# A two-layer graph kernel: layer 1's buffers laid over early-ending ones, off-diagonal sources first, denominators in pairs, P three deep

## The chip, the core and the metric

The kernel runs on one core of a Trainium2 chip. The time is that of the device for one launch, in microseconds (us); a kernel is timed in several runs and the median is given. A profile of one run shows what each engine did: PE (TensorE; PEld is its weight loads), DVE (VectorE), ACT (ScalarE), POOL (GpSimd) and SP (SyncE, which here only issues transfers).

## What is computed

There are N = 2708 nodes with D = 256 features. Layer 0 is two steps of a top-p attention and of a random walk, with residuals and two layer norms. It stands ahead of the change and is not given here. Layer 1 is a graph attention with H = 4 heads of FO = 64 features:

```python
Wh = jnp.einsum('nd,hdo->nho', x, W)
s_i = jnp.einsum('nho,ho->nh', Wh, a_src)
s_j = jnp.einsum('nho,ho->nh', Wh, a_dst)
e = leaky_relu(s_i[:, None, :] + s_j[None, :, :], 0.2)
mask = (adj_with_unit_diagonal != 0)[:, :, None]
attention = softmax(where(mask, e, -inf), axis=1)
h_prime = jnp.einsum('ijh,jho->iho', attention, Wh)
x = layernorm(x + h_prime.reshape(n, h * fo))
```

For each target node i, every source node j is weighted by exp(leaky_relu(s_i + s_j)) where the adjacency isn't zero. The diagonal always counts.

## The kernel before, in words

The 2708 nodes are 22 tiles: 16 of 128 rows and 6 of 110. `fast_layer0` computes layer 0 with an order of instructions written out by hand. As each tile t of layer 0's result is ready, `sources(t)` multiplies it with the weights and leaves the scaled values of that tile as a DRAM tensor `vd[t]` (line 160), and in SBUF `sb` = exp(s_j), `tj` = exp(-0.8 s_j) and `s_src` = s_i. Each pool of layer 0 is opened where it is first used, and all are closed before layer 1. (A slower general path for layer 0 follows under a condition that isn't met with these inputs.)

`layer1` uses that exp(leaky_relu(s_i + s_j)) divided by exp(0.2 s_i) is exp(s_j) · max(exp(0.8 s_i), exp(-0.8 s_j)), and that the divisor cancels in the softmax. So for a source tile j and head h

P_h = max(r_h, tj_h) · mask,

with r = exp(0.8 s_i) spread over all partitions, one column for each target. Values are v(j) transposed times P, denominators `bj(j)` transposed times P, with `bj` = sb repeated 32 times.

Targets come in three spans of 8, 8 and 6 tiles (1024, 1024 and 660 columns). In each span a loop goes over all 22 source tiles:

- `neighbours` (lines 1131 to 1143): the `bar` transfer (L1136) brings the 128 rows of the transposed adjacency, issued on SP; ACT takes the Sign (L1137); if tile j is itself in the span, POOL sets the diagonal to one (L1140, L1141); ACT takes the Square (L1142). Four `bar` buffers.
- Four DVE operations make P for the four heads (L1189), in the pool `pj` with two buffers for each head.
- PE adds the values to `acc[0]` and `acc[1]` (L1197), two heads at a time side by side in column tiles 64 wide. It then adds the denominators to `acc[2]` (L1204), four heads side by side in column tiles 32 wide. In the profile each of these matmuls leaves two records.

At the span's end, ACT and DVE copy the sums to SBUF (L1212 to L1214). `settle` then finishes the span's tiles one by one: three PE transposes (L1152, L1153), the reciprocal and the product on DVE (L1155, L1159), the residual on POOL (L1164), the layer norm on DVE and POOL (L125 to L132), and the transfer to the output. It stands in the program at the third source (j == 2) of the next span; the last span's comes at the end. `targets(g + 1)` (PE transposes L1122, ACT exponentials L1126) makes the next span's r at j == 11.

The values of all 22 sources are loaded from `vd` at the head of `layer1`, issued on ACT (L1103); POOL makes the 22 `bj` (L1104).

Two things set the order around the change. A scheduler puts each engine's instructions in order from the program's order and from its dependences. And the pools set addresses: a buffer of layer 1 lies over some buffer of layer 0, and what writes it first waits for that one's last reader. Before the change, `bar` lies over the buffers `xa1` and `hh` of layer 0's last sums and norms, r over `yw` and `ba`, v and bj over weights and row buffers, and the transposes' `aux` banks over those of `att` and `walk`.

Of the kernel before, what the change touches and what calls it, by code (L numbers as in the profile page):

```python
# [8 lines left out]
F32 = mybir.dt.float32  # L9
# [5 lines left out]
PSUM = bass.MemoryType.PSUM  # L15
# [30 lines left out]
def kernel(  # L46
# [407 lines left out]
    def fast_layer0():  # L454

        l0 = ExitStack()
        w0 = l0.enter_context(tc.tile_pool(name="w0", bufs=1))
        rowp = l0.enter_context(tc.tile_pool(name="rowp", bufs=2))
        keep = l0.enter_context(tc.tile_pool(name="keep", bufs=1))
        HN = N // 2  # L460
# [11 lines left out]
        b_sb = w0.tile([P, D], F32, name="b_sb")  # L472
        heldp = l0.enter_context(tc.tile_pool(name="heldp", bufs=HELD))
        tmp = heldp.tile([P, D], F32, name="xa1")
# [41 lines left out]

        qT = keep.tile([P, N], F32, name="qT")
        yw = keep.tile([P, NT, D], F32, name="yw")
        ba = keep.tile([P, NT, D], F32, name="ba")
        rinv = keep.tile([P, NT], F32, name="rinv")  # L520

        dram = l0.enter_context(tc.tile_pool(name="dram", bufs=1, space=bass.MemoryType.DRAM))
        c1 = [dram.tile([P, D], F32, name=f"c1_{t}") for t in range(NT)]
        c2 = [dram.tile([P, D], F32, name=f"c2_{t}") for t in range(NT)]

        sortp = l0.enter_context(tc.tile_pool(name="sortp", bufs=1))
        finp = l0.enter_context(tc.tile_pool(name="finp", bufs=2))
        ep = l0.enter_context(tc.tile_pool(name="ep", bufs=3))
        wk = l0.enter_context(tc.tile_pool(name="wk", bufs=1))

        kT = [wk.tile([P, HN], F32, name="junk"), keep.tile([P, HN], F32, name="kT1")]
        tpp = l0.enter_context(tc.tile_pool(name="tpp", bufs=3))
        adjp = l0.enter_context(tc.tile_pool(name="adjp", bufs=3))
        ps_lg = l0.enter_context(tc.tile_pool(name="ps_lg", bufs=2, space=PSUM))
        ps_tr = l0.enter_context(tc.tile_pool(name="ps_tr", bufs=2, space=PSUM))
        ps_at = l0.enter_context(tc.tile_pool(name="ps_at", bufs=1, space=PSUM))
        ps_wk = l0.enter_context(tc.tile_pool(name="ps_wk", bufs=1, space=PSUM))

# [551 lines left out]
    def layer1():  # L1090
        l1 = ExitStack()
        keep = l1.enter_context(tc.tile_pool(name="keep1", bufs=1))
        pp = l1.enter_context(tc.tile_pool(name="pp", bufs=2))
        GT = 8
# [3 lines left out]

        v = [keep.tile([P, H, FO], F32, name=f"v{t}") for t in range(NT)]
        bj = [keep.tile([P, H, 32], F32, name=f"bj{t}") for t in range(NT)]  # L1100
        for t in range(NT):
            m = rows[t]
            nc.scalar.dma_start(v[t][:m].rearrange("p h o -> p (h o)"), vd[t][:m])  # L1103
            nc.gpsimd.tensor_copy(  # L1104
                bj[t][:m], sb[:m, t, :].unsqueeze(2).to_broadcast([m, H, 32])
            )

        rp = l1.enter_context(tc.tile_pool(name="rp", bufs=2))
        adjp = l1.enter_context(tc.tile_pool(name="adjp1", bufs=4))
        pj = l1.enter_context(tc.tile_pool(name="pj", bufs=2))  # L1110
        ps_v = l1.enter_context(tc.tile_pool(name="ps_v", bufs=1, space=PSUM))
        ps_u = l1.enter_context(tc.tile_pool(name="ps_u", bufs=2, space=PSUM))

# [57 lines left out]
        for g, span in enumerate(spans):  # L1171
# [5 lines left out]
            ]  # L1177
            for j in range(NT):
                k = rows[j]
                if j == 2 and due:  # L1180
                    settle(*due)
                if j == NT // 2 and g + 1 < len(spans):
                    r_next = targets(g + 1)
                mask = neighbours(g, j)
                at = dict(start=(j == 0), stop=(j == NT - 1), skip_group_check=True)
                pts = []
                for h in range(H):
                    pt = pj.tile([P, GW], F32, name=f"pt{h}")
                    nc.vector.scalar_tensor_tensor(  # L1189
                        pt[:k, :gw], r[:k, h, :gw], tj[:k, j, h : h + 1], mask,  # L1190
                        op0=ALU.max, op1=ALU.mult,
                    )
                    pts.append(pt)
                    if h % 2 == 1:
                        for c, (c0, w) in enumerate(cuts):
                            for q in range(2):
                                nc.tensor.matmul(  # L1197
                                    acc[h // 2][c][q * FO : (q + 1) * FO, :w],
                                    v[j][:k, h - 1 + q, :],
                                    pts[h - 1 + q][:k, c0 : c0 + w], **at,  # L1200
                                )
                for c, (c0, w) in enumerate(cuts):
                    for h in range(H):
                        nc.tensor.matmul(  # L1204
                            acc[2][c][h * 32 : (h + 1) * 32, :w],
                            bj[j][:k, h, :], pts[h][:k, c0 : c0 + w], **at,
                        )
            r = r_next
# [61 lines left out]
```

The softmax here doesn't subtract the row's maximum and nothing guards it: scores larger than these inputs give would overflow.

## Time and profile before

| | |
|---|---|
| time, median of 3 runs | 1698.4 us (1698.17 to 1698.85) |
| span of the profiled run | 1697.3 us |
| PE busy | 1620.3 us (95%) |
| DVE busy | 1219.5 us (72%) |
| ACT busy | 767.9 us (45%) |
| POOL busy | 433.6 us (26%) |
| last attention matmul of layer 0 (L187) | starts at 1277.08, 2.75 us |
| last layer norm of layer 0 (L909) | 1289.91, 0.41 us |
| first value product of span 1, 2, 3 | 1312.03, 1439.06, 1576.65 us |
| values of the last source of span 3 | 1671.46 us |

The page gives busy time in 40 slices of the span (tenths), then groups of instructions: line, engine, operation, output and inputs by name, and how many; then busy time and mean ns of one; then the idle time of the engine just ahead of them and what ended most of it. A row of the timeline has start, duration, engine, line, operation, output and inputs, count, and in brackets the idle time before it with its releaser. "SPq" and "ACTq" rows are issues of transfers. In a table by windows each engine's busy time stands with its count, followed by the clock granted to PE, the busy share of the DMA engines and GB/s.

### The profile page before, as it was taken

Reading aid. Unit: us, or ns where it says so; the run is one execution under the profiler, and the core shown is the slowest. Engines: PE = TensorE matmul, PEld = TensorE weight load, DVE = VectorE, ACT = ScalarE, POOL = GpSimd, SP = SyncE. Lnnn points to the kernel's source line nnn. Section 1 sums busy time; section 2 is a strip of 40 time slices with the busy share of each in tenths; the row PEclk is TensorE's granted clock in tenths of the full one; section 3 lists DMA queues with packets and bytes.
Section 4 is the critical chain, followed back from the end, with each engine's and each line's share of the span. In section 5 each row is a group of like instructions: output and inputs, shape, how many; then the busy total and the mean of one; then the engine's idle time right before and its main releaser. Section 6 shows DMA issues by size and latency. Waiting matters only on the chain. (4 is left out here: it accounts for less than half of the span.)

```text
span 1697.3 us, 24178 instructions
## 1 busy us (share of the span) xinstructions
PE 1620.3 (95%) x8306; PEld 1064.8 (63%) x8306; DVE 1219.5 (72%) x3660; ACT 767.9 (45%) x1324; POOL 433.6 (26%) x915
## 2 busy tenths in 40 slices
PE   7999999999999999999999999999985999999895
PEld 4677777777767766777878788777773232322332
DVE  2954554556445029888899999998981989889886
ACT  1333333333333256566666767676723444243231
POOL 0310111111101033223344444453434200430312
PEclk9999999999999999999999999999996999999997
DMA  6211011101111133122223323322204323232231
GB/s 164 72 46 46 27 41 39 43 27 39 40 42 40 44 89 77 48 67 75 71 74 82 85 65 87 80 71 66 68 22 126 100 82 94 87 86 78 73 85 31
DMA packets 153873, 113.89 MB, mean 67 GB/s; under 512 B 39898, under 2 KB 144094, under 8 KB 153742
## 3 DMA queue, kind: packets, MB, share of 16 engines
q1 hardware_dynamic: 146248, 102.41, 22.7%
q0 software_dynamic: 2112, 5.55, 1.0%
q10 hardware_dynamic: 5382, 4.32, 0.9%
q8 instruction: 67, 1.10, 0.3%
q14 instruction: 64, 0.52, 0.1%
HBM read 101.16 MB, written 11.09 MB: 66 GB/s over the span
## 5 line engine op out<-in xcount | busy, mean ns | idle before, releaser
L1189 DVE SCALAR_TENSOR_TENSOR pt<-r,tj,bar 128x1024 f32<-128x1024 f32 (+3 forms) x264 | 297.0, 1187 | 49.8 <-ACT bar L1142 25.5
L619 ACT ACTIVATE junk<-e,minus,rth 128x2708 bf16<-128x2708 f32 (+1 forms) x88 | 233.0, 2648 | 36.1 <-POOL rth L651 35.3
L819 PE MATMUL walk<-xe,blk 128*128 128x257 f32 (+3 forms) x968 | 240.6, 382 | 0.0
L187 PE MATMUL att<-ba,eT 128*128 128x256 f32 (+3 forms) x968 | 234.4, 383 | 5.0 <-ACT eT L178 5.0
L187 PE MATMUL att<-xe,eT 128*128 128x256 f32 (+3 forms) x968 | 233.3, 381 | 4.3 <-ACT eT L178 4.3
L1197 PE MATMUL acc<-pt,v 128*64 128x512 f32 (+3 forms) x1056 | 230.5, 554 | 4.6 <-DVE pt L1189 4.6
L178 ACT COPY eT<-tr 128x512 f32<-128x512 f32 (+5 forms) x264 | 138.2, 538 | 203.3 <-PE tr L172 203.0
L819 PE MATMUL walk<-yw,blk 128*128 128x256 f32 (+3 forms) x968 | 228.0, 381 | 1.8 <-ACT xw L889 1.8
L699 DVE MAX8 cand<-e 128x8 f32<-128x170 f32 (+1 forms) x352 | 89.3, 324 | 171.5 <-ACT e L598 171.5
L819 PEld LDWEIGHTS walk<-xe,blk 128*128 128x128 f32 (+3 forms) x968 | 173.0, 186 | 53.1 <-issue 29.3
L819 PEld LDWEIGHTS walk<-yw,blk 128*128 128x128 f32 (+3 forms) x968 | 176.7, 186 | 41.6 <-issue 11.5
L187 PEld LDWEIGHTS att<-ba,eT 128*128 128x128 f32 (+3 forms) x968 | 171.9, 187 | 33.0 <-ACT eT L178 10.0
L187 PEld LDWEIGHTS att<-xe,eT 128*128 128x128 f32 (+3 forms) x968 | 170.8, 186 | 30.9 <-ACT eT L178 7.2
L598 ACT ACTIVATE e<-lg 128x1024 f32<-128x1024 f32 (+1 forms) x132 | 121.1, 922 | 132.3 <-PE lg L594 132.3
L1197 PEld LDWEIGHTS acc<-pt,v 128*64 128x64 f32 (+1 forms) x1056 | 73.7, 137 | 154.8 <-issue 111.9
L172 PE MATMUL tr<-ident,e 128*128 128x128 f32 (+3 forms) x968 | 140.5, 269 | 4.6 <-ACT xT L580 3.8
L172 PEld LDWEIGHTS tr<-ident,e 128*128 128x128 f32 (+3 forms) x968 | 115.0, 138 | 32.7 <-ACT xT L580 6.1
L1137 ACT ACTIVATE bar<-bar 128x1024 f32<-128x1024 f32 (+3 forms) x66 | 63.0, 956 | 146.0 <-DMA bar<-in_adjT_dram 110.1
L1204 PE MATMUL acc<-pt,bj 128*32 128x512 f32 (+3 forms) x1056 | 124.5, 549 | 0.0
L605 POOL TENSOR_TENSOR fact<-zp 128x1 f32<-128x1 f32 (+1 forms) x44 | 24.9, 566 | 329.2 <-ACT e L598 319.4
L699 DVE MAX8 cand<-scr 128x8 f32<-128x97 f32 (+1 forms) x616 | 101.9, 247 | 0.0
L832 DVE TENSOR_TENSOR xf<-walk,xe 128x257 f32<-128x257 f32 (+1 forms) x22 | 9.4, 427 | 117.4 <-PE walk L819 117.3
(199 smaller groups left out, 2022.1 us busy)
## 6 DMA issues: line engine op xcount, KB each, us to landing
blk<-in_adjT_dram SPq DMA_DIRECT2D x32, 704.0 KB
bar<-in_adjT_dram SPq DMA_DIRECT2D x32, 512.0 KB
blk<-in_adjT_dram SPq DMA_DIRECT2D x32, 330.0 KB
blk<-in_adjT_dram SPq DMA_DIRECT2D x32, 320.0 KB
blk<-in_adjT_dram SPq DMA_DIRECT2D x12, 605.0 KB
bar<-in_adjT_dram SPq DMA_DIRECT2D x12, 440.0 KB
bar<-in_adjT_dram SPq DMA_DIRECT2D x16, 330.0 KB
c<-cs POOLq DMA_DIRECT2D x32, 128.0 KB, 2.1
```

What stands on the lines that cost most here:

```text
L172: nc.tensor.transpose(tr[: rows[t], q, :m], e[:m, off[t] : off[t + 1]], ident[:m, :m])
L178: copy(eT[:k, : len(grp), :m], tr[:k, : len(grp), :m])
L187: nc.tensor.matmul(acc, eT[: rows[t], q, :m], value(t), start=(t == 0), stop=(t == NT - 1),)
L598: nc.scalar.activation(halves[:m, :, c0 : c0 + w], lg[:m, :, :w], AF.Exp, accum_out=zp[:m, n : n + 1],)
L605: nc.gpsimd.tensor_add(z, zp[:m, 0:1], zp[:m, 1:2])
L619: nc.scalar.activation(junk[:m], e[:m], func, scale=rth, bias=minus1[:m], accum_out=acc)
L699: nc.vector.max(cand[:, n, :], src[:m, n * size : min(N, (n + 1) * size)])
L819: nc.tensor.matmul(ac[:m, :w], blk[: rows[j], j - j0, :m], cur[: rows[j], j, 0:w], start=(j == 0), stop=(j == NT - 1),)
L1137: nc.scalar.activation(bar, bar, AF.Sign)
L1189: nc.vector.scalar_tensor_tensor(pt[:k, :gw], r[:k, h, :gw], tj[:k, j, h : h + 1], mask, op0=ALU.max, op1=ALU.mult,)
L1197: nc.tensor.matmul(acc[h // 2][c][q * FO : (q + 1) * FO, :w], v[j][:k, h - 1 + q, :], pts[h - 1 + q][:k, c0 : c0 + w], **at,)
L1204: nc.tensor.matmul(acc[2][c][h * 32 : (h + 1) * 32, :w], bj[j][:k, h, :], pts[h][:k, c0 : c0 + w], **at,)
```

## The change

It has four parts.

1. **Pools laid over each other.** Layer 0 opens its pools in one list, layer 1 in another, in an order that lays layer 1's first buffers over those of layer 0 that end early. After it `bar` lies over `blk` and `e`, r over `e`, P over `ba`, `kT1`, `qT` and `cand`, the v of the first sources over `yw`, and `acc` and `aux` over PSUM banks of `lg`, `walk`, `att` and `tr`. This is to let layer 1 begin while layer 0's last tiles go through their norms.
2. **Off-diagonal sources first.** The first span takes sources 8 to 19, then 0 to 7, then 20 and 21. Those of its own tiles, which need POOL for the diagonal, come later. Each source's v is loaded and its bj copied in the loop, just ahead of its mask, and the load is issued on SP instead of ACT. In the other spans the order stays.
3. **Denominators of two sources in a row.** The values of j and of j + 1 come first, then the denominators of both. PE changes between the two tile widths half as often.
4. **P three deep.** Each head's P has three buffers; with pairs, one source's P is held while the next one's values are computed.

The core of the diff:

```diff
-        w0 = l0.enter_context(tc.tile_pool(name="w0", bufs=1))
-        rowp = l0.enter_context(tc.tile_pool(name="rowp", bufs=2))
-        keep = l0.enter_context(tc.tile_pool(name="keep", bufs=1))
+        heldp, finp, rowp, w0, keep, sortp, adjp, ep, tpp, wk = (
+            l0.enter_context(tc.tile_pool(name=name, bufs=bufs))
+            for name, bufs in (
+                ("heldp", HELD), ("finp", 2), ("rowp", 2), ("w0", 1), ("keep", 1),
+                ("sortp", 1), ("adjp", 3), ("ep", 3), ("tpp", 3), ("wk", 1),
+            )
+        )
+        ps_lg, ps_wk, ps_at, ps_tr = (
+            l0.enter_context(tc.tile_pool(name=name, bufs=bufs, space=PSUM))
+            for name, bufs in (("ps_lg", 2), ("ps_wk", 1), ("ps_at", 1), ("ps_tr", 2))
+        )
...
     def layer1():
         l1 = ExitStack()
-        keep = l1.enter_context(tc.tile_pool(name="keep1", bufs=1))
-        pp = l1.enter_context(tc.tile_pool(name="pp", bufs=2))
+        pp, keep, pj, adjp, rp = (
+            l1.enter_context(tc.tile_pool(name=name, bufs=bufs))
+            for name, bufs in (("pp", 2), ("keep1", 1), ("pj", 3), ("adjp1", 4), ("rp", 2))
+        )
+        ps_u = l1.enter_context(tc.tile_pool(name="ps_u", bufs=2, space=PSUM))
+        ps_v = l1.enter_context(tc.tile_pool(name="ps_v", bufs=1, space=PSUM))
...
-        v = [keep.tile([P, H, FO], F32, name=f"v{t}") for t in range(NT)]
-        bj = [keep.tile([P, H, 32], F32, name=f"bj{t}") for t in range(NT)]
-        for t in range(NT):
+        v, bj = {}, {}
+        for t in reversed(range(NT)):
+            v[t] = keep.tile([P, H, FO], F32, name=f"v{t}")
+            bj[t] = keep.tile([P, H, 32], F32, name=f"bj{t}")
+
+        def stationary(t):
             m = rows[t]
-            nc.scalar.dma_start(v[t][:m].rearrange("p h o -> p (h o)"), vd[t][:m])
+            nc.sync.dma_start(v[t][:m].rearrange("p h o -> p (h o)"), vd[t][:m])
             nc.gpsimd.tensor_copy(
                 bj[t][:m], sb[:m, t, :].unsqueeze(2).to_broadcast([m, H, 32])
             )
-        rp = l1.enter_context(tc.tile_pool(name="rp", bufs=2))
-        adjp = l1.enter_context(tc.tile_pool(name="adjp1", bufs=4))
-        pj = l1.enter_context(tc.tile_pool(name="pj", bufs=2))
...
-            for j in range(NT):
+            order = list(range(NT)) if g else list(range(GT, NT - 2)) + list(range(GT)) + [NT - 2, NT - 1]
+            waiting = []
+            for n, j in enumerate(order):
                 k = rows[j]
-                if j == 2 and due:
+                if n == 2 and due:
                     settle(*due)
-                if j == NT // 2 and g + 1 < len(spans):
+                if n == NT // 2 and g + 1 < len(spans):
                     r_next = targets(g + 1)
+                if g == 0:
+                    stationary(j)
...
-                for c, (c0, w) in enumerate(cuts):
-                    for h in range(H):
-                        nc.tensor.matmul(
-                            acc[2][c][h * 32 : (h + 1) * 32, :w],
-                            bj[j][:k, h, :], pts[h][:k, c0 : c0 + w], **at,
-                        )
+                waiting.append((j, k, pts, at))
+                if n % 2 == 1:
+                    for j, k, pts, at in waiting:
+                        for c, (c0, w) in enumerate(cuts):
+                            for h in range(H):
+                                nc.tensor.matmul(
+                                    acc[2][c][h * 32 : (h + 1) * 32, :w],
+                                    bj[j][:k, h, :], pts[h][:k, c0 : c0 + w], **at,
+                                )
+                    waiting = []
```

The rest of the diff only takes out the lines where the listed pools stood and moves one tensor (`qT`) behind two others.

## The prediction

> **What bounds the kernel now.** I read the page first (shares, then groups), then the busy time by windows, then the timeline of three stretches: the change of layers, the steady loop of layer 1, and the loop while the previous span is settled.
>
> The page, sections 2 and 5 (busy time, mean ns of one, idle time ahead):
>
> ```profile
> PE   7999999999999999999999999999985999999895
> ...
> L1189 DVE SCALAR_TENSOR_TENSOR pt<-r,tj,bar 128x1024 f32<-128x1024 f32 (+3 forms) x264 | 297.0, 1187 | 49.8 <-ACT bar L1142 25.5
> ...
> L1197 PE MATMUL acc<-pt,v 128*64 128x512 f32 (+3 forms) x1056 | 230.5, 554 | 4.6 <-DVE pt L1189 4.6
> ...
> L1204 PE MATMUL acc<-pt,bj 128*32 128x512 f32 (+3 forms) x1056 | 124.5, 549 | 0.0
> ```
>
> TensorE (PE) is full but for the first slice, slices 30 and 31 (42.4 us each: 1231 to 1315, the change from layer 0 to layer 1), 38 (the third span's start) and 40 (the last settle). The 264 P products of VectorE (DVE, L1189) are the second load of layer 1. By windows (us, PE, PEld, DVE, ACT, POOL busy, clock, DMA):
>
> ```profile
> 1280.00:1300.00 20.00, 11.95 (x49) 8.19 (x48) 3.46 (x9) 8.56 (x32) 10.83 (x25) 0.74 0.42 130
> 1300.00:1350.00 50.00, 39.94 (x210) 12.83 (x212) 38.49 (x30) 21.51 (x23) 17.24 (x28) 0.83 0.42 125
> 1350.00:1400.00 50.00, 50.00 (x296) 15.01 (x296) 41.27 (x35) 20.49 (x23) 0.00 (x0) 1.00 0.29 82
> ```
>
> From 1350 PE is the bound; before that it starves. The timeline there shows why:
>
> ```profile
> 1290.40 0.36 SPq L1136 DMA_DIRECT2D bar<-in_adjT_dram  x1
> ...
> 1297.55 11.04 ACTq L1103 DMA_DIRECT2D v<-v  x21
> ...
> 1308.63 1.09 ACT L1126 ACTIVATE r<-aux 128x512 f32<-128x512 f32 x2 [10.67 <-DMA v<-v]
> ...
> 1310.69 2.68 DVE L1189 SCALAR_TENSOR_TENSOR pt<-r,tj,bar 128x1024 f32<-128x1024 f32 x2 [20.37 <-ACT bar L1142]
> ...
> 1312.03 1.97 PE L1197 MATMUL acc<-pt,v 128*64 128x512 f32 x2 [0.78 <-DVE pt L1189]
> ```
>
> The first `bar` transfer leaves at 1290.40, when the last layer norm of layer 0 (DVE L909, 1289.91 + 0.41) has let its buffer go. ACT then issues v loads for 11.04 us, and the last two exponentials `r` (1308.63), the Square of the first mask (1309.60) and the first P (1310.69) queue behind. PE's first value product is at 1312.03; two sources are through at 1326.09.
>
> The steady loop:
>
> ```profile
> 1347.85 3.65 PE L1197 MATMUL acc<-pt,v 128*64 128x512 f32 x16
> 1347.99 4.87 DVE L1189 SCALAR_TENSOR_TENSOR pt<-r,tj,bar 128x1024 f32<-128x1024 f32 x4 [0.56 <-issue]
> 1348.33 0.14 PEld L1197 LDWEIGHTS acc<-pt,v 128*64 128x64 f32 x2 [0.29 <-issue]
> ...
> 1351.43 0.16 PEld L1204 LDWEIGHTS acc<-pt,bj 128*32 128x32 f32 x8 [0.81 <-issue]
> ...
> 1353.28 0.20 PEld L1197 LDWEIGHTS acc<-pt,v 128*64 128x64 f32 x4 [0.84 <-DVE pt L1189]
> ```
>
> A source takes 5.44 us (1347.85 to 1353.28; 5.439 over 1320.65 to 1433.62, after 4.2 for the transposes of `targets`). Weight loads follow each other every 0.4286, twelve steps, 5.143. The other 0.295 lies at the two switches between 64-wide values and 32-wide denominators: there PEld idles 0.81 and 0.84, elsewhere 0.29. DVE needs 4.87, then waits 0.56 for the denominators to free P.
>
> While the previous span is settled (second span, 1450 to 1476):
>
> ```profile
> 1462.27 0.41 DVE L132 TENSOR_SCALAR o<-res,ln_mv,ln_rs 128x256 f32<-128x256 f32 x1 [0.46 <-POOL ln_rs L131]
> 1462.59 0.75 DVE L1159 TENSOR_TENSOR res<-aux,rden 128x256 f32<-128x256 f32 x2
> ...
> 1463.26 1.64 DVE L1189 SCALAR_TENSOR_TENSOR pt<-r,tj,bar 128x1024 f32<-128x1024 f32 x1
> ...
> 1468.80 1.55 DVE L1189 SCALAR_TENSOR_TENSOR pt<-r,tj,bar 128x1024 f32<-128x1024 f32 x1
> ```
>
> One P per 5.5 us, with two tiles settled between: DVE makes 8 P in 26 us, where PE could use 19.
>
> **What the Trainium skill says.**
> - "TensorEngine Tiling (Array Packing)", Key Properties: a change of tiling mode drains TensorE. The trace agrees: 0.147 us per switch.
> - "DMA: Bandwidth & Descriptors", Issuing engines are not separate DMA queues: a different issuing engine saves sequencer time only. The trace shows that time: 11.04 us of ACT for 21 issues, 0.53 each.
> - "TensorE: Matmul & The Clock Gate", What's actually happening: after an idle window TensorE runs at half clock until it has been busy some 3.4 us. It agrees in kind: clock 0.74 and 0.83 in the windows above, and the first source's values take 6.84 against 3.65 (some of this is waiting for P).
> - "SBUF — State Buffer", SBUF: two separate sides: a DVE operation with two SBUF inputs and a GpSimd operation lock each other out. It agrees: a P takes 1.22 alone, 1.317 over the first 24 (POOL masks the diagonal), up to 1.64 at 1463.
>
> **The change, part by part.** Instruction counts are equal but for 22 issues moved from ACT to SP, and the built order is the same up to the last 30 us of layer 0. So layer 0 stays.
>
> *Change of layers.* The masks now lie over buffers (blk, e) whose last readers, transposes of the last e, are through at about 1277, so `bar` leaves some 13 us earlier. In ACT's new order the first Sign and Square stand between r(0) and r(5); what ends last is r(6) and r(7), behind the last cs of layer 0 (ACT, ends 1294.87): two exponentials with their transposes, 1.5 to 2.2, so the first P at about 1296.7, 14 earlier. The first sources are off-diagonal: no POOL work, P at 1.22. The first v lies over yw and also needs the store of v_21 (issued 1294.90; 2.1 to land, as c<-cs): loads start near 1297.5 and land near 1300. PE's first denominators wait for bj, copied by POOL then. Values of source 8 from 1300.3 to 1304.8 (part cold), of 9 to 1308.8, remaining denominators 3 to 3.5: two sources through at 1312.5 against 1326.1. Gain 13.5; 11 if the clock starts cold later, 15 if nothing waits for v.
>
> *Pairs.* v(j) v(j+1) d(j) d(j+1) has 2 switches in 4 segments, where there were 4: 0.147 saved per source. First span: 20 sources, 2.9, less 0.5 while diagonal sources keep DVE at 5.27 against the new period of 5.29: 2.4. Second: 22, 3.2, less 0.7: 2.5. P(j) is now held until d(j), so P(j+3) waits for d(j): in a pair's 10.58 the two denominators end at 9.0 and 10.8, DVE then makes its two sources in 9.74, and values need them at 14.2 and later. I cost this wait at nothing.
>
> *P three deep, settle.* From 1439.06 to 1488.69, six sources took 49.6; six periods (32.6), 5.4 of settle transposes and 1.9 of `targets` make 40: 9.6 lost to DVE. In the new order DVE starts on settle half a source earlier, but spreads it: one tile (1.51) to one P (1.25 to 1.6), ten P over the eight tiles. P runs at 2.8 to 3.2 with one more source in store (5.3 of PE work). Walking it through leaves 2 to 5 lost: gain 4.6 to 7.6, taken 6.1. Third span (660 wide): period 3.618, values 2.37, denominators 1.25, DVE 3.36; seven sources took 44.15 against 30.7. There the order still has two tiles per P but starts two or three P later. Counting the same way eight sources end 42.9 after the start against 47.8: 4.9 with switches; 14 other sources save 0.147 each, 2.1, less 1 on the last six diagonal ones (DVE 3.63 against 3.47): 6.0, from 3 to 8.
>
> *At no cost.* The v issues on SP: it only issues loads, 0.5 each, 22 in 118 us. The bj copies (0.24) lie on POOL behind layer 0's norms and ahead of masks needed a source later. The last settle (about 22 us) is as before: denominators are still last.
>
> Sum: 13.5 + 2.4 + 2.5 + 6.1 + 6.0 = 30.5. 1698.4 − 30.5 = 1667.9, say 1668.
>
> **Rivals.**
> - *DVE becomes the bound* (15%). For it: 5.27 per diagonal source against 5.29, and P up to 1.64 beside POOL. Against: 41.27 of 50 busy off the diagonal. Pairs give nothing, settle its low ends: 13.5 + 4.6 + 3 = 21, 1677.
> - *The start is only half gained* (17%). For it: a source's v comes through a store, SP and a load, one after the other, and PE is cold. Gain 6.5 instead of 13.5: 1675.
> - *Slower* (3%). SP is one queue in order; each v issue stands ahead of its mask, behind a mask load that waits for a buffer. Were every source of the first span to pay one landing (2.1, as c<-cs), 22 × 2.1 = 46 less 30.5: 1714. Against: four masks in flight are 16 us of lead.
>
> **How the numbers follow.** The main case has 65%. Adding low ends (11 + 1 + 1 + 4.6 + 3) gives 20.6, high ends (15 + 2.9 + 3.2 + 7.6 + 8) 36.7: 1662 to 1678. The range reaches from 1660 to 1682, which takes in both milder rivals (1675 and 1677) with some 6 us for a low end more; the slower case and worse mixes are left out. Faster 0.96, within 0.2% 0.01, slower 0.03.
>
> **What would show it.** First `bar` issue near 1277, first P near 1297, first value product near 1300; starts of segments 10.6 apart for two sources with half the 0.8 marks of PEld; six sources at the second span's start in about 43; layer 1's last settle as long as now. Wrong if ACT waits for `bar` or PE for v in the first span, if DVE waits for d at P with POOL beside it, or if layer 0 ends later than 1280.

## The result, and the profile after

The changed kernel takes 1690.3 us (median of 4 runs, 1689.55 to 1690.42), the kernel before 1698.4 in the same session: a ratio of 0.9951, 95% interval 0.9934 to 0.9968. That is 8.1 us faster. 30.5 were forecast, and the time lies outside the range of 1660 to 1682.

The page of the changed kernel, sections 2 and 5. The lines of code have moved by some six: P is L1195, values L1203, denominators L1214.

```profile
PE   7999999999999999999999999999998989899995
...
L1195 DVE SCALAR_TENSOR_TENSOR pt<-r,tj,bar 128x1024 f32<-128x1024 f32 (+3 forms) x264 | 293.0, 1176 | 39.4 <-issue 19.5
...
L1203 PE MATMUL acc<-pt,v 128*64 128x512 f32 (+3 forms) x1056 | 223.1, 549 | 4.0 <-DVE pt L1195 4.0
...
L1214 PE MATMUL acc<-pt,bj 128*32 128x512 f32 (+3 forms) x1056 | 122.5, 545 | 0.9 <-POOL bj L1110 0.9
```

The dip at slices 30 and 31 is nearly gone (it was 8 and 5, it is 9 and 8), but there is a new dip in slice 33, in the middle of the first span, and another in slice 35, where the second span begins; PE was full in both before. By windows:

```profile
1280.00:1300.00 20.00, 13.21 (x62) 9.05 (x61) 6.43 (x12) 14.67 (x40) 9.74 (x17) 0.83 0.37 132
1300.00:1350.00 50.00, 50.00 (x276) 14.71 (x274) 47.37 (x40) 20.67 (x21) 25.72 (x22) 1.00 0.48 142
1350.00:1400.00 50.00, 45.00 (x266) 14.80 (x264) 36.03 (x31) 18.78 (x21) 14.44 (x15) 0.93 0.26 82
```

From 1300 to 1350 PE now works all 50 us instead of 39.9. From 1350 to 1400 it works 45 where it worked 50. The timeline of the change of layers:

```profile
1277.99 0.36 SPq L1136 DMA_DIRECT2D bar<-in_adjT_dram  x1
...
1297.03 33.34 DVE L1195 SCALAR_TENSOR_TENSOR pt<-r,tj,bar 128x1024 f32<-128x1024 f32 x27 [5.97 <-ACT r L1126]
...
1298.59 2.98 PE L1214 MATMUL acc<-pt,bj 128*32 128x512 f32 x8 [0.90 <-POOL bj L1110]
...
1301.50 7.46 PE L1203 MATMUL acc<-pt,v 128*64 128x512 f32 x32
...
1312.45 5.37 PE L1203 MATMUL acc<-pt,v 128*64 128x512 f32 x24
```

The first mask leaves at 1277.99 instead of 1290.40. The first P starts at 1297.03 instead of 1310.69, behind the last r on ACT. Two sources are through at 1312.45 instead of 1326.09. The steady loop of pairs:

```profile
1377.67 0.20 PEld L1203 LDWEIGHTS acc<-pt,v 128*64 128x64 f32 x4 [0.84 <-DVE pt L1195]
1377.67 7.09 PE L1203 MATMUL acc<-pt,v 128*64 128x512 f32 x32
...
1384.69 0.16 PEld L1214 LDWEIGHTS acc<-pt,bj 128*32 128x32 f32 x8 [0.81 <-issue]
1384.69 3.64 PE L1214 MATMUL acc<-pt,bj 128*32 128x512 f32 x32
...
1388.26 0.20 PEld L1203 LDWEIGHTS acc<-pt,v 128*64 128x64 f32 x4 [0.84 <-DVE pt L1195]
```

A pair takes 10.59 us (1377.67 to 1388.26), 5.29 for a source, with two gaps of 0.8 where there were four.

So both the start and the pairs do what they were forecast to do. Where the 22 us went is seen when the timeline is cut into stages. "Two through" is the time at which two sources' values and denominators are done. A span starts with its first value product. The last one ends with its last denominators, less the 0.07 by which neighbouring matmuls overlap in the trace, so that all spans are counted from start to start.

| | two through | rest of span 1 | span 2 | span 3 | last settling to the end |
|---|---|---|---|---|---|
| before | 1326.1 | 113.0 | 137.6 | 98.4 | 22.2 |
| after | 1312.5 | 118.2 | 139.9 | 95.9 | 22.0 |
| difference | −13.6 | +5.2 | +2.3 | −2.5 | −0.2 |

The sum is −8.8, the difference of the profiled spans (1697.3 and 1688.5).

**The first span** loses in one place. One pair, from 1355.92 to 1377.67, takes 21.75 instead of 10.59. It holds the transposes of `targets` (n == 11), which cost 4.2 by themselves; 7.0 are lost. The timeline of that pair:

```profile
1354.35 9.77 DVE L1195 SCALAR_TENSOR_TENSOR pt<-r,tj,bar 110x1024 f32<-110x1024 f32 x8 [0.53 <-issue]
...
1358.78 5.66 POOL L1140 TENSOR_TENSOR bar<-bar,offdiag 128x128 f32<-128x128 f32 x1 [4.10 <-ACT bar L1137]
...
1365.01 1.06 ACT L1142 ACTIVATE bar<-bar 128x1024 f32<-128x1024 f32 x1 [6.31 <-POOL bar L1141]
1365.97 1.07 ACT L1126 ACTIVATE r<-aux 128x512 f32<-128x512 f32 x2
1366.60 1.97 PE L1122 MATMUL aux<-ident,s_src 128*128 128x128 f32 x8 [5.00 <-ACT r L1126]
...
1370.23 0.46 POOL L1140 TENSOR_TENSOR bar<-bar,offdiag 128x128 f32<-128x128 f32 x1 [5.25 <-ACT bar L1137]
1370.37 1.09 PE L1122 MATMUL aux<-ident,s_src 128*128 128x128 f32 x8
...
1376.10 9.65 DVE L1195 SCALAR_TENSOR_TENSOR pt<-r,tj,bar 128x1024 f32<-128x1024 f32 x8 [11.98 <-issue]
```

Read from the bottom of the wait up. PE has two PSUM buffers for the transposes and stands at the third (5.00). ACT hasn't emptied them, since a Square stands ahead of r in its queue, and that Square waits 6.31 for POOL. POOL's small product on the diagonal takes 5.66 instead of 0.46 (1370.23, with no P beside it), and ends as DVE's run of eight P ends (1364.12). In the new order the diagonal sources come at n == 12 and after, just behind `targets`. The wait is 5.00 of the 7.0. The rest comes after it: from 1363.5 to 1370.2 the clock granted to PE was 0.50, where the kernel before has 1.00, and eight transposes take 1.97 at 1366.60 and 1.09 at 1370.37.

**The second and third span** lose while the previous span is settled. The first eight sources of the second span take 59.9 us. Four pairs and 5.4 of transposes make 47.7, so 12.2 are lost, where the kernel before lost about 9.6. In the third span 14.1 are lost (before: 13.4). The timeline of two tiles, second span:

```profile
1457.77 1.26 DVE L1195 SCALAR_TENSOR_TENSOR pt<-r,tj,bar 128x1024 f32<-128x1024 f32 x1
1457.77 1.84 POOL L1164 TENSOR_TENSOR res<-res,xe 128x256 f32<-128x256 f32 x1 [1.19 <-DVE ln_mv L127]
...
1459.88 0.57 POOL L131 TENSOR_TENSOR ln_rs<-ln_ve,minus_half 128x1 f32<-128x1 f32 x1
...
1460.49 0.41 DVE L132 TENSOR_SCALAR o<-res,ln_mv,ln_rs 128x256 f32<-128x256 f32 x1 [1.47 <-POOL ln_rs L131]
...
1461.63 1.25 DVE L1195 SCALAR_TENSOR_TENSOR pt<-r,tj,bar 128x1024 f32<-128x1024 f32 x1
```

One tile and one P take 3.86 us (1457.77 to 1461.63). DVE is idle for 1.47 of them: its `o` waits for POOL's `ln_rs`, which stands behind the next tile's residual, and that takes 1.84 beside a P. Over the eight tiles DVE waits 11.3 us for POOL. In the third span the order is as before, two tiles to one P, and so is the wait, 6.3. In the kernel before it was 6.3 in the second span too. This is the wait of the first of two tiles there:

```profile
1461.39 0.41 DVE L132 TENSOR_SCALAR o<-res,ln_mv,ln_rs 128x256 f32<-128x256 f32 x1 [0.80 <-POOL ln_rs L131]
```

### The profile page after: what moved, and what is told of

Its sections match the earlier page's. It is cut to its first block, busy times and chain, and to the rows that moved or that the text cites. A ratio compares the mean times of both kernels' runs of the same rounds, so it can differ in the third digit from the quotient of the medians.

```text
span 1688.5 us, 24169 instructions
## 1 busy us (share of the span) xinstructions
PE 1614.1 (96%) x8306; PEld 1069.7 (63%) x8306; DVE 1214.4 (72%) x3660; ACT 767.5 (45%) x1324; POOL 455.7 (27%) x915
## 5 line engine op out<-in xcount | busy, mean ns | idle before, releaser
L1195 DVE SCALAR_TENSOR_TENSOR pt<-r,tj,bar 128x1024 f32<-128x1024 f32 (+3 forms) x264 | 293.0, 1176 | 39.4 <-issue 19.5
L1203 PE MATMUL acc<-pt,v 128*64 128x512 f32 (+3 forms) x1056 | 223.1, 549 | 4.0 <-DVE pt L1195 4.0
L1203 PEld LDWEIGHTS acc<-pt,v 128*64 128x64 f32 (+1 forms) x1056 | 73.9, 137 | 145.2 <-issue 110.9
L1214 PE MATMUL acc<-pt,bj 128*32 128x512 f32 (+3 forms) x1056 | 122.5, 545 | 0.9 <-POOL bj L1110 0.9
```

Of the source, the lines that this page charges most:

```text
L1195: nc.vector.scalar_tensor_tensor(pt[:k, :gw], r[:k, h, :gw], tj[:k, j, h : h + 1], mask, op0=ALU.max, op1=ALU.mult,)
L1203: nc.tensor.matmul(acc[h // 2][c][q * FO : (q + 1) * FO, :w], v[j][:k, h - 1 + q, :], pts[h - 1 + q][:k, c0 : c0 + w], **at,)
L1214: nc.tensor.matmul(acc[2][c][h * 32 : (h + 1) * 32, :w], bj[j][:k, h, :], pts[h][:k, c0 : c0 + w], **at,)
```

## The experiments

All kernels here compute what the kernel before does. Each time is a median, with the ratio to the kernel before, timed beside it, and its 95% interval. Stages are as above; the first line repeats the changed kernel. In the names, "np" is without pairs, "away" has the stage with r moved away from n == 11, "deep" has P four deep, "spread" and "light" settle in another way.

| | time, us | ratio (interval) | two through | rest of span 1 | span 2 | span 3 |
|---|---|---|---|---|---|---|
| after | 1690.3 | 0.9951 (0.9934–0.9968) | 1312.5 | 118.2 | 139.9 | 95.9 |
| t_away | 1681.1 | 0.9900 (0.9884–0.9917) | 1311.1 | 111.2 | 138.6 | 95.9 |
| no_pair | 1683.2 | 0.9913 (0.9896–0.9929) | 1310.7 | 113.7 | 139.5 | 94.4 |
| pools_only | 1685.0 | 0.9920 (0.9904–0.9937) | 1312.3 | 113.2 | 137.6 | 98.0 |
| natural | 1688.3 | 0.9940 (0.9924–0.9957) | 1313.1 | 114.7 | 141.5 | 95.9 |
| np_away | 1677.2 | 0.9875 (0.9859–0.9892) | 1312.4 | 113.0 | 133.2 | 94.4 |
| deep4 | 1681.7 | 0.9903 (0.9886–0.9920) | 1311.5 | 117.3 | 139.7 | 89.7 |
| deep4_away | 1676.9 | 0.9874 (0.9857–0.9890) | 1311.7 | 111.2 | 139.9 | 89.7 |
| np_spread | 1676.3 | 0.9873 (0.9857–0.9889) | 1310.3 | 113.0 | 135.3 | 93.1 |
| r_by_tile | 1666.8 | 0.9819 (0.9802–0.9835) | 1310.3 | 109.5 | 132.6 | 89.7 |
| spread | 1674.1 | 0.9858 (0.9842–0.9875) | 1311.5 | 109.5 | 137.0 | 91.5 |
| spread_light | 1656.4 | 0.9756 (0.9739–0.9772) | 1311.0 | 109.5 | 123.7 | 85.8 |
| spread_light_np | 1660.2 | 0.9777 (0.9761–0.9794) | 1312.0 | 111.9 | 126.4 | 83.4 |
| light_only | 1688.1 | 0.9942 (0.9925–0.9958) | 1312.4 | 118.1 | 137.5 | 97.1 |
| deep_light | 1671.9 | 0.9844 (0.9828–0.9861) | 1311.8 | 109.5 | 131.6 | 94.9 |
| hybrid | 1651.9 | 0.9730 (0.9714–0.9747) | 1311.7 | 109.5 | 123.7 | 83.4 |

### Which part of the change did what

**t_away** moves the stage with r to where no diagonal source follows.

```diff
-                if n == NT // 2 and g + 1 < len(spans):
+                if n == (6, 18, 0)[g] and g + 1 < len(spans):
                     r_next = targets(g + 1)
```

> The changed kernel with one edit: the next span's r (the targets stage) is made at n == 6 of the first span and n == 18 of the second, instead of n == 11, so that it stands among off-diagonal sources. Theory A (at n == 11 the transposes stand beside the first diagonal source; POOL's mask waits for DVE's run of P, ACT's Square for POOL, ACT's r for the Square, PE for r): the pair of sources with these transposes takes about 15 us instead of 21.8, the second span starts 7 us earlier, total about 1683. The built order also changes on DVE at the second span's settle: it starts one whole source later and with two tiles to one P; if the settle's loss is set by that order, 3 to 6 more, 1677 to 1680. Rival B (the diagonal sources are simply slow for DVE and POOL): the first span stays as long, total 1690.

The first span became 7.0 us shorter, as theory A had it: the two pairs that share the transposes take 25.4, which is two periods and 4.2. The second span became 1.3 shorter, at its own stage with r, and the third kept its time. The other half of the expectation wasn't put to the test. In the trace DVE settles the second span in the same order as in the changed kernel, one tile to one P from the same source on, and the first eight sources take the same 59.9. So this run says nothing about what that order costs.

**no_pair** takes the pairs back and keeps the three buffers, **pools_only** takes both back.

```diff
-                if n % 2 == 1:
+                if True:
                     for j, k, pts, at in waiting:
```
```diff
-            for name, bufs in (("pp", 2), ("keep1", 1), ("pj", 3), ("adjp1", 4), ("rp", 2))
+            for name, bufs in (("pp", 2), ("keep1", 1), ("pj", 2), ("adjp1", 4), ("rp", 2))
```

> The changed kernel with pairs undone: each source's denominators follow its values at once; P stays three deep. By the cost of a switch, 0.147 us, the period of the first two spans goes back from 5.29 to 5.44 and the third's from 3.47 to 3.62: 9 us dearer in all. Theory A: the stall at n == 11 has nothing to do with pairs and stays, 5 to 7 us. If the settle's loss comes from DVE's order (one tile to one P, which the pairs brought; here it is two tiles to one P, one source later), the second span's first eight sources lose 5 to 7 instead of 12: total about 1692. If the settle's loss doesn't depend on the order: 1699.

> The changed kernel with pairs undone and P two deep again: only the buffers laid over each other, the first span's order and the v loads on SP are left. Two sources should be through near 1312.5 (before: 1326.1), a gain of 13.6. Theory A: at n == 11 the stall costs 5 to 7, total 1690 to 1692. If the stall needs the three deep P or the pairs (a run of eight P on DVE): no stall, total 1685. Settle as in the kernel before (9.6 and 13.4 lost).

Pools, order and v loads alone bring 13.3 of time (1698.3 to 1685.0), more than the whole change. Their spans are those of the kernel before. Three deep P without pairs brings 1.8 more; with pairs on top the kernel is 7 us slower. no_pair shows why it isn't better: its second span loses only 4.3 while settling (ten sources in 64.0 us, against 54.4 + 5.4), where pools_only, with the same order on DVE and one buffer less, loses 9.7. So the third buffer does there what was forecast. In the first span both have hardly a stall, against theory A: the pair with the transposes loses 0.2 in pools_only and 0.8 in no_pair. So the new order alone doesn't make it; it comes with pairs and the longer run of P on DVE. But in its second span no_pair loses 7.0 at n == 11, where that span has its diagonal sources (8 to 15), with PE again 4.86 us behind ACT's r.

**natural** keeps everything but the first span's order.

```diff
-            order = list(range(NT)) if g else list(range(GT, NT - 2)) + list(range(GT)) + [NT - 2, NT - 1]
+            order = list(range(NT))
```

> The changed kernel with the first span's sources in natural order, 0 to 21; all else as changed. Theory A: at n == 11 the sources are off-diagonal, so the stall of 7 us is gone. The start has diagonal sources: P at 1.3 instead of 1.2 and masks through POOL while it makes bj, 1 to 4 us later for the first two sources. Total 1684 to 1688. Rival B (diagonal sources cost the same wherever they stand): 1690 or more.

Two sources are through at 1313.1, only 0.6 later: the start isn't won by the order. Whether by the buffers or by the v loads, which every kernel but the one before issues on SP, no run tells apart. The trace of before gives an estimate. There ACT's last two r and the first Square stand behind 11.04 us of v issues (1297.55 to 1308.59), while the first mask's Sign has ended at 1296.99 and the transposes for those r at 1298.67. Without the issues the first P could have come near 1300.4 instead of 1310.69, which is some 10 of the 13.6; the other 3 would be the earlier masks. The next two pairs take 12.5 and 13.2 instead of 11.7 and 10.6, and the pair with the transposes 14.9. So the order saves 4 us early and, together with pairs, costs 7 at n == 11.

### How much P is in store

**np_away** is no_pair with t_away's edit. **deep4** is the changed kernel with a fourth buffer, **deep4_away** both together.

```diff
-            for name, bufs in (("pp", 2), ("keep1", 1), ("pj", 3), ("adjp1", 4), ("rp", 2))
+            for name, bufs in (("pp", 2), ("keep1", 1), ("pj", 4), ("adjp1", 4), ("rp", 2))
```

> The changed kernel with pairs undone, P three deep, and the next span's r made at n == 6 of the first span and n == 18 of the second. With pairs undone alone, the second span lost 7.0 us at n == 11, where its diagonal sources are (8 to 15), and 4.3 while settling. Theory A (the stage with r must not stand beside diagonal sources): those 7 go, the first span stays, total 1676. Rival B (the 7 us belong to the recovery of DVE after settling, not to the place of r): no gain, 1683.

> The changed kernel with P four deep instead of three, pairs as changed. Theory C (a pair holds one source's P until its late denominators, so that of three buffers no more is in store than of two without pairs): with the fourth the loss while settling falls from 12.2 to about 4 in the second span and from 14 to 9 or 10 in the third, as three deep without pairs has it; total 1690 - 12 = 1678 if the stall at n == 11 stays, 1671 if that goes too. Rival D (the loss while settling is one of DVE's order, or of POOL's locked port): 1688 to 1690.

> Both: P four deep with pairs, r made at n == 6 and n == 18. Theories A and C together: 1681 - 12 = 1669. If depth does nothing: 1681.

np_away came out as theory A had it (1677.2 for 1676): the second span is 6.4 shorter and the third as it was. Under pairs the fourth buffer cuts the loss of settling from 12.2 to 7.1 in the second span and from 14.1 to 7.9 in the third, 11 together, where 12 were expected. So a pair does use up a buffer: three with pairs hold no more in store than two without.

The same numbers give an estimate of what DVE's order costs. In the second span, kernels with two tiles to one P lose 9.7 (pools_only) and 4.3 (no_pair), those with one tile to one P and, so counted, the same store 12.2 (after) and 7.1 (deep4). A buffer is worth 5.1 to 5.4, one source of PE's work, and the order 2.5 to 2.8. No run changes the order alone.

The second span of deep4 took as long as before all the same, 139.7: what settling gave back went at n == 11, where its pair takes 21.3 instead of 16.4. And deep4_away didn't reach 1669. Its second span kept a loss of 7.7, now at n == 18, where no source is diagonal:

```profile
1535.10 0.75 ACT L1137 ACTIVATE bar<-bar 128x660 f32<-128x660 f32 x1 [3.23 <-DMA bar<-in_adjT_dram]
...
1536.54 0.95 ACT L1126 ACTIVATE r<-aux 128x440 f32<-128x440 f32 x2
1537.12 1.73 PE L1122 MATMUL aux<-ident,s_src 110*128 110x110 f32 x8 [4.39 <-ACT r L1126]
...
1550.59 1.72 DVE L1195 SCALAR_TENSOR_TENSOR pt<-r,tj,bar 128x660 f32<-128x660 f32 x2 [8.89 <-issue]
```

PE is at n == 18, ACT already at masks of the next span (660 wide), and r is queued behind one whose transfer hadn't come. POOL plays no part. The stall is one of order on ACT: r stands behind masks that wait for something. On the diagonal that is POOL, here a transfer. That ACT's queue runs further ahead of PE's when more P is in store fits these runs, but was not measured by itself.

**r_by_tile** has four buffers and makes r one tile at a time, so that no third tile's transposes stand right behind those of two others.

```diff
-                if n == NT // 2 and g + 1 < len(spans):
-                    r_next = targets(g + 1)
+                first = (1, 15, 0)[g]
+                if g + 1 < len(spans) and first <= n < first + len(spans[g + 1]):
+                    r_next = targets(g + 1, r_next if n > first else None, n - first)
```

> P four deep with pairs, and the next span's r made one tile at a time: eight tiles at n = 1 to 8 of the first span, six at n = 15 to 20 of the second. With all tiles at once PE sat behind ACT's third exponential, which stood behind the Sign and Square of a mask several sources ahead: 6 to 8 us lost in each of the two spans with four deep P at n == 11 (1681.7), one such stall of 7.7 left with r at n == 6 and 18 (1676.9). Theory G (only the third tile of a row has to wait, since the transposes have two PSUM buffers): one tile at a time never waits, 1669. Rival H (what PE loses there is DVE's debt from settling, and shows up anywhere): 1676.

1666.8, near what theory G gave (1669), and 7.3 less in the second span than deep4_away. The first span's rest, 109.5, is now what ten pairs and 4.2 of transposes make (110.1): nothing is lost there.

### What settling costs

**np_spread** is np_away (with r at n == 20) with settling one tile at a time, at n = 2, 4, ... 16 (PLACES); **spread** is r_by_tile with the same edit.

```diff
-                if n == 2 and due:
-                    settle(*due)
+                if due and n in PLACES:
+                    settle(*due, only=PLACES.index(n))
```

> The changed kernel with pairs undone, P three deep, r made at n == 6 and n == 20, and the previous span settled one tile at a time, at n = 2, 4, ... 16, instead of all eight at n == 2. Theory E (settling loses time since DVE can't make P for a stretch longer than what is in store): DVE has 9.74 for two P sources and 1.5 for a tile, against PE's 10.88 and 0.67, so nearly nothing is lost: 2 in the second span and 3 in the third instead of 4.3 and 9.4; total 1676 - 9 = 1667. Rival F (each tile costs DVE its wait for POOL too, 1.4 us, and diagonal sources leave DVE no room): 1672 to 1680.

> As r_by_tile, and the previous span settled one tile at a time at n = 2, 4, ... 16. DVE's sum in the second span is 88 P at 1.22, 3 for the diagonal, 12 to settle and 6 of waits for POOL, 129, against PE's 116.5 + 8.5 = 125 with pairs; in the third 74.4 + 2 + 12 + 5 = 93 against 82. Theory I (DVE is the bound of spans two and three once PE has pairs): spreading helps only by what it saves of waits: second span 131 to 134, third 88 to 91; total 1661 to 1667. Rival J (PE stays the bound): second span 127, third 84, total 1655.

Spreading alone doesn't help in total. Against np_away, np_spread gained 1.4 in the third span and lost 2.2 in the second, and spread is 7 us slower than r_by_tile. At first it does what theory E said: the first ten sources of the second span take 55.3 in `spread` and 65.5 in r_by_tile, and all that their pairs cost over the period is the transposes. Then two losses take it back. At diagonal sources (n = 10 to 13) DVE is the bound: in `spread` a pair takes 12.6 (1476.3 to 1501.6), in which DVE works or waits for POOL all the time. And r is late once more. PE waits 4.07 for it in np_spread, where it stands at n == 20 behind masks whose transfers are late, and 7.12 in `spread`, though r is made by tile there:

```profile
1525.75 0.99 PE L1123 MATMUL aux<-ident,s_src 110*128 110x110 f32 x4 [7.12 <-ACT r L1127]
```

The waits of DVE in the second span of `spread` (total, times, longest):

```profile
DVE ln_st L125 <- POOL res L1167: 7.3, 8, 2.0
DVE o L132 <- POOL ln_rs L131: 6.2, 8, 0.8
DVE pt L1199 <- ACT r L1127: 5.0, 1, 5.0
```

**spread_light** takes those waits from DVE. Product and residual become one DVE operation for each head, and the last step of the norm goes to POOL.

```diff
-                nc.vector.tensor_tensor(
-                    res[:m], u[:m, 0:2, :].rearrange("p q (h o) -> p (q h) o", h=2),
-                    rden[:m].unsqueeze(2).to_broadcast([m, H, FO]), op=ALU.mult,
-                )
-                nc.gpsimd.tensor_add(flat, flat, xe[:m, t, 0:D])
+                for h in range(H):
+                    nc.vector.scalar_tensor_tensor(
+                        res[:m, h, :], u[:m, h // 2, (h % 2) * FO : (h % 2 + 1) * FO],
+                        rden[:m, h : h + 1], xe[:m, t, h * FO : (h + 1) * FO],
+                        op0=ALU.mult, op1=ALU.add,
+                    )
...
-            nc.vector.tensor_scalar(dst, src, mv[:m, 0:1], rs[:m], op0=ALU.subtract, op1=ALU.mult)
+            nc.gpsimd.tensor_scalar(dst, src, mv[:m, 0:1], rs[:m], op0=ALU.subtract, op1=ALU.mult)
```

> As spread, with less of settling on DVE: the product and the residual are one DVE operation for each head (four of 64 columns), and the last step of the norm is on POOL. DVE works about 1.2 us for a tile instead of 1.5 and waits for POOL nowhere. Theory I: DVE's sum falls by 8 in each of spans two and three, and the time by 5 to 10 against spread. Rival K (POOL's port is locked by P, so that its last step comes late and holds the output, or slows P): the same as spread, or up to 3 slower.

17.7 us faster than `spread`, more than expected. The second span is 123.7 where 116.5 for eleven pairs and 8.5 for transposes make 125. The two waits for POOL are gone from the list. The one wait for r that is left is the same; it is DVE's at the first P of the third span, when the second span's P are all made:

```profile
DVE pt L1213 <- ACT r L1127: 5.0, 1, 5.0
DVE pt L1213 <- PE acc L1232: 2.0, 3, 1.0
```

DVE's work isn't less: 116.44 us busy in its second span, 116.10 in that of `spread` (windows of 123.7 and 137.0, the lengths of the two spans). What fell is its waiting. Of the 13.3 that the second span gained, 8.9 are in the one pair where PE had stood behind r (20.7 in `spread`, 11.8 here) and the rest in the three pairs ahead of it. That r came late in `spread` because DVE was late is likely, but not shown. Spread_light changes two things of `spread` at once, so it doesn't tell either which of DVE's two waits for POOL mattered.

**spread_light_np** is the same without pairs.

> As spread_light, with pairs undone (P four deep, r by tile, settling spread and light). PE's sum is 9 larger over the three spans (0.147 for each of 66 sources, less the last). Theory I says pairs are worth nothing where DVE is the bound: 0 to 4 slower than spread_light, nearly all in the first span. Rival J (PE the bound): 8 to 9 slower.

3.8 slower: 2.4 in the first span's rest and 2.7 in the second are PE's switches come back. The third span is 2.4 faster without pairs: its 83.4 are 22 periods of 3.62 and 3.8 for the transposes, so nothing is lost. With pairs 5.5 are, nearly all in the last four sources (18 to 21, on the diagonal). There DVE waits for the mask, and the mask for POOL, which now also has the last step of the norm:

```profile
1612.66 0.75 ACT L1143 ACTIVATE bar<-bar 110x660 f32<-110x660 f32 x1 [3.69 <-POOL bar L1142]
...
1613.45 3.52 DVE L1213 SCALAR_TENSOR_TENSOR pt<-r,tj,bar 110x660 f32<-110x660 f32 x4 [1.52 <-ACT bar L1143]
```

**light_only** puts only the light settling of the first two spans into the changed kernel, **deep_light** into r_by_tile; all eight tiles stay at n == 2.

> The changed kernel with one edit, in settling of the first two spans: product and residual are one DVE operation for each head, and the last step of the norm is on POOL, so that DVE doesn't wait for POOL. Pairs, three deep P, r at n == 11 and settling at n == 2 stay. Theory L (what settling loses is DVE's wait for POOL, whose residual is locked out while a P runs: 1.4 us for a tile, at each of the tiles): the second span loses 2 to 5 while settling instead of 12.2, the third 4 to 7 instead of 14.1; the stalls with r stay; total 1671 to 1676. Theory C alone (too little P in store under pairs, whatever the waits): 1684 to 1688.

> P four deep with pairs, r by tile (1666.8), and light settling of the first two spans, all eight tiles at n == 2. Theory L: 1666.8 less 5 to 8 in the second span and 3 to 6 in the third: 1653 to 1658, no worse than settling tile by tile (1656.4, which had 2.7 of its time in a slower last settling on POOL). If tile by tile is needed too: 1660 to 1664.

Both were far from theory L: light_only is 2.2 faster than the changed kernel (their intervals overlap), deep_light 5.1 slower than r_by_tile. The timeline of light_only shows that the edit did not do what it was made for:

```profile
1451.28 1.24 POOL L1154 TENSOR_SCALAR o<-res,ln_mv,ln_rs 128x256 f32<-128x256 f32 x1
...
1452.56 0.28 DVE L1181 SCALAR_TENSOR_TENSOR res<-aux,rden,xe 128x64 f32<-128x64 f32 x1 [1.33 <-POOL o L1154]
```

With eight tiles in a row DVE has to wait for POOL's `o` to free one of two `res` buffers, 1.33 for a tile in place of 1.4. And the order on DVE has seven tiles behind each other with no P between: after the P at 1442.01 the next starts at 1461.56. So these two don't tell what the wait alone is worth; they show that taking one wait away gains little when it brings another, and when no P is made for 18 us.

**hybrid** is spread_light with the last span's settling as it was and no pairs in the third span.

```diff
-                if n % 2 == 1:
+                if n % 2 == 1 or g == 2:
                     for j, k, pts, at in waiting:
...
-                layernorm(o[:m], flat, m)
+                (layernorm if g == 2 else settled)(o[:m], flat, m)
```

> spread_light with two edits: the last span's settling is as in the kernel before (its POOL form made the end 2.7 us longer), and the third span has no pairs (83.4 us without, 85.8 with). Expected: 1656.4 - 2.7 - 2.4 = 1651.3.

1651.9, as added up, 46 us below the kernel before and 38 below the changed one. Its second and third span by windows:

```profile
1421.20:1545.00 123.80, 123.80 (x758) 39.17 (x754) 116.56 (x148) 47.25 (x54) 56.71 (x40) 1.00 0.31 93
1545.00:1628.40 83.40, 83.40 (x733) 34.16 (x729) 76.00 (x137) 26.77 (x39) 40.36 (x36) 1.00 0.26 75
```

PE is busy from the second span's start to the third's end.

## Why the prediction was wrong

Direction, the times of the start and the price of a switch were right; the size was 22 us off. Three steps failed: the longer hold of P was costed "at nothing", `targets` kept its old price of 4.2 in the new order, and DVE's pace while settling was summed from its work, without its waits.

- **Change of layers: right in size, its cause in part open.** 13.5 forecast, 13.6 measured. The first P came at 1297.03 (1296.7), the first value product at 1301.50 (1300.3), two sources were through at 1312.45 (1312.5). That the end fits so well has some luck in it: the values began 1.2 late and then took 7.46 for two sources, at full clock, where 8.5 were forecast. pools_only confirms the gain in time, 13.3, and the rival with half of it is out. But the forecast gave the gain to the earlier masks and listed the v issues on SP under "no cost". By the estimate above most of it may be that move.
- **Pairs: price right, the cost of holding P missing.** 0.147 for each source held: 5.29 and 3.475 are the measured periods. But the step that costed the longer hold of P "at nothing" looked only at the steady loop. There it is nothing. While DVE settles it takes away what is in store: one buffer more (deep4) took 11 us off the losses of settling, though 5 of them went again at n == 11.
- **First span: 2.4 faster forecast, 5.2 slower measured.** The step took `targets` over at its old price, 4.2. It never asked what stands beside it in the new order. n == 11 had been off-diagonal and now borders on the diagonal sources; PE waits behind ACT's r, that behind a Square, that behind POOL, that behind DVE's run of P. The order on ACT was there to be seen. t_away gave the 7.0 back. It takes the new order and pairs together: where one of them is missing (the order in natural, pairs in no_pair and pools_only), 0.1 to 0.8 are lost at this place. That the port lock is the first link is read from the trace alone; deep4_away shows that the stall comes by another first link too.
- **Settling, second span: 6.1 faster forecast, 2.6 slower measured** (2.7 more at its own n == 11). Two assumptions failed. "P runs at 2.8 to 3.2" summed DVE's work; it ran at 3.86, since `o` waits 1.4 for POOL at nearly each tile. That wait could have been read before: the line of `o` that the prediction shows has 0.46 of idle time for POOL, the one of the tile ahead of it 0.80 (shown above), and in an order of tile, P, tile the P would meet POOL's residual. "One more source in store" was wrong under pairs: the changed kernel lost 12.2, deep4 7.1. no_pair lost 4.3, within the 2 to 5 of the forecast, but with two tiles to one P, which is not the order that the forecast walked through.
- **Third span: 6.0 forecast, 2.5 measured.** The switches gave 3.1; settling lost 14.1 instead of 13.4, and the first eight sources took 46.2 where 42.9 were forecast. Here DVE's order and its waits for POOL stayed as before, so what failed is the store alone: deep4 lost 7.9.
- **The rivals.** "DVE becomes the bound" was nearest. It was not its busy time, as the rival had it (5.27 against 5.29 at the diagonal; the pairs there ran at 10.59), but its waits and the P that it had not in store. The range left out that two such losses can come together: 8.1 us faster is the start's gain of 13.6 with 5.5 taken back.

What stays open: no run moved the pools without the v issues, so the start's 13.6 isn't divided between them. The wait for POOL in settling was only taken away together with spreading (spread_light), so its share by itself, with eight tiles at n == 2, isn't known. The 1.1 us that the second pair of the first span takes more (11.71) is where PE has one denominator matmul among the pair's values, by itself and with two more switches (1317.75 to 1318.72); no run was made on it.

## What to carry to other kernels

When two users of a buffer are put in a row, count the buffers in store at the moment of the longest other work, not in the steady loop: a pair needed a fourth buffer to have about what three gave without it. When loop iterations are reordered, look at what stands at a fixed iteration number beside them, on every in-order queue. And price small side work on a busy engine by the time from one of the main operations to the next, waits included: from `spread` to spread_light DVE's work stayed at 116 us in the second span, its waits for POOL went, and the kernel became 17.7 us faster.

## What was not expected of the hardware

POOL's 128x128 product took 5.66 us beside a run of eight P on DVE, ending 0.3 after the run did, against 0.46 where no P ran. The Trainium skill, "SBUF — State Buffer", SBUF: two separate sides, has the exclusive lock, and the trace agrees. What it means was not foreseen: with P back to back POOL isn't slowed by a share, it may be held out for the whole run. It isn't always: in spread_light such a product took 1.43 (1486.14) inside a run of five P, which took 6.37, where 6.03 is seen for the next five. What decides isn't shown. The residual, 128x256, took 1.74 to 1.84 beside one P and 0.72 in `spread` where it began after one had ended.
